# Turning the row maxima with one transpose and placing them by transfers, in an attention and expert-layer kernel

## The chip, the cores and the metric

The kernel runs on one core of a Trainium2 chip. A core has five engines with a queue of instructions each: TensorE (PE in the profile; PEld is its loading of weights), VectorE (DVE), ScalarE (ACT), GpSimd (POOL) and SyncE (SP), which here only issues transfers (DMAs). Each engine takes its own queue in order and waits at semaphores for the others. SBUF is the working memory with 128 partitions, PSUM holds the matmul results in banks. The metric is the time on the device in microseconds: 559.02 us, the median of three runs (559.01 to 559.05).

## What is computed

A layer of attention and then a mixture of experts, each followed by a residual sum and a layer norm, on x of 2 x 1024 x 256, all in float32. What matters here is the attention: 16 query heads of 16 elements share 4 key heads, a bias that grows linearly with the key's position is added, a causal mask, then softmax:

```python
q = (x @ Wq).reshape(B, T, N_HEAD, HEAD_DIM).transpose(0, 2, 1, 3)
k = (x @ Wk).reshape(B, T, N_HEAD_KV, HEAD_DIM).transpose(0, 2, 1, 3)
v = (x @ Wv).reshape(B, T, N_HEAD_KV, HEAD_DIM).transpose(0, 2, 1, 3)
...
att = jnp.einsum('bhqd,bhkd->bhqk', q, k) * scale
...
att = att + alibi[None]
...
att = att + causal[None, None]
att = jax.nn.softmax(att.astype(jnp.float32), axis=-1).astype(q.dtype)
y = jnp.einsum('bhqk,bhkd->bhqd', att, v)
y = y.transpose(0, 2, 1, 3).reshape(B, T, C)
return y @ Wo
```

The second half routes each token to one of 8 experts (top 1) and adds a shared expert; the change touches of it only the place where its first loads are issued.

## The kernel before

**Tiles.** There are 2 batches of 8 query tiles with 128 queries each, 16 in all, worked through as tiles 0 to 7 of batch 0 and then 7 to 0 of batch 1 (`order`). For query tile qt there are qt + 1 key tiles, so 72 steps (b, qt, kt). Each step is two slots, one for each half h of the four key heads.

**The operands.** `qT[b]` holds the queries turned, [128 partitions, 4 repeats r, 1024 tokens]: each key head g owns 32 partitions, of which row 16 and on hold the 16 elements of a head, row 0 (`ROW_POS`) serves the position bias, and row 1 (`ROW_MAX`) is for the maximum. `kT[b]` has the matching rows, with ones in `ROW_MAX`. So a matmul over the 32 partitions adds whatever stands in the query's row 1 to every score.

**Scores twice.** The scores are computed once with queries on partitions (`start_s`, line 427, tile `s_ps`), only to find each row's maximum: `end_s` reduces them on DVE (`past`, line 446), and takes the block on the diagonal to `diag` on DVE (line 459) or ACT (line 461), POOL masks it, and DVE reduces it later as a "chore" (line 478). Row 1 of `qT` is zero for this. Then they are computed again with keys on partitions (`start_t`, line 519, tile `t_ps`), now with the negated maximum in row 1; `end_t` takes exp of them on ACT (`pT`, line 538), or for the diagonal block copies them (`pD`, line 541), masks on POOL and takes exp (line 555). `product` (line 565) multiplies by v.

**Between the two.** `join_maxima` (line 492) joins the partial maxima of a tile into `mneg` on DVE; `spread_maxima` turns them on PE (line 503) and adds them to a copy of the queries, `qS`, on DVE (line 507), which `start_t` reads.

**The order.** It is written out by hand: all five engines run in program order (`manual_schedule`). The maxima run ahead of the exponentials by `LEAD` = 10 units, which run first, among the projections of the remaining tokens (`do_q` and others, from `fill`). Then each slot is a burst of t and s matmuls in turn, t0, s0, t1, s1, followed by `gap`, with one product, the joining or spreading of maxima (`maxima`), one piece of the work behind a finished tile (`posts`: yq, ytp, o_ps, x1tp, lg) and one chore. For tile k with its first step at slot 2*first, `join_maxima` runs in the gap of slot 2*first - 4, `spread_maxima` in that of 2*first - 3; the bursts of slots 2*first - 2 and 2*first - 1 lie between it and the first t matmuls of the tile. A slot whose spreading put it into `with_chore` runs no chore. When the maxima are all done (`s_queue` empty), `wide_gap` puts pieces of the shared expert (gu_sh, dp_sh) between bursts.

**Buffers.** s_ps, t_ps and most other matmul results share one pool of 6 PSUM banks; yT has one bank, and mT shares the last one with yq, ytp, o_ps and others (tag "m").

**Transfers.** `do_q` (line 358) issues 8 DMAs of 64 KB on SP for each 512 tokens, 32 in all, from SBUF to `qT` within SBUF. Behind the `LEAD` units, SP issues the loads of the shared expert's weights (lines 932 to 934) and fills the DRAM tables `slot_x` and `more_x` with one empty row repeated (line 941). Their next instructions on SP are the stores of `z_sh` (line 764), at the end of the attention. ACT issues the loads of Wq, Wk and Wv at the start, and nothing else before the expert stage. `slot` starts at -10, so that the spreading of tile 0 falls in slot -3 (behind the query transfers of batch 1's first half, before those of its second) and of tile 1 in slot -1, behind all of them.

Of the kernel before, what the change touches and what calls it, by code (L numbers as in the profile page):

```python
# [9 lines left out]
F32 = mybir.dt.float32  # L10
I32 = mybir.dt.int32
# [5 lines left out]
P = 128  # L17
N_HEAD = 16
N_KV = 4
REP = N_HEAD // N_KV  # L20
HD = 16
PAD = 32
ROW_POS = 0
ROW_MAX = 1
# [21 lines left out]
def attn_moe_postln_kernel(  # L46
# [15 lines left out]
    nc = tc.nc  # L62
    B, T, C = x.shape
    E, _, F2 = gate_up.shape
    FF = F2 // 2
# [3 lines left out]
    NTT = B * QT  # L69
# [9 lines left out]
    ROW = C + 4  # L79
    NUM, WT = C, C + 1  # L80
# [10 lines left out]
    acon = attn_scope.enter_context(tc.tile_pool(name="acon", bufs=1))  # L91
# [19 lines left out]
    sh_gu = const.tile([P, KC, F2], F32, tag="sh_gu", name="sh_gu")  # L111
    sh_d = const.tile([P, FC, C], F32, tag="sh_d", name="sh_d")

    mnegs = []
    for i in range(2):
        m = acon.tile([P, REP, N_KV, PAD], F32, tag=f"mneg{i}", name=f"mneg{i}")
        nc.gpsimd.memset(m, 0.0)
        mnegs.append(m)  # L120
    ident = const.tile([P, P], F32, tag="ident", name="ident")
    make_identity(nc, ident)
    neg_half = const.tile([P, 1], F32, tag="neg_half", name="neg_half")
# [25 lines left out]
    for g, slope in enumerate(alibi_slopes()):  # L149
# [14 lines left out]
        out=causal,  # L164
        in_=causal,
# [9 lines left out]
    for b in range(B):  # L175
# [15 lines left out]
        out=before,  # L191
        in_=ones,
# [75 lines left out]
    with (  # L268
# [12 lines left out]
        qT, kT, xT = {}, {}, {}  # L281
# [5 lines left out]
        def own_tiles(b, xTb):  # L287
            xT[b] = xTb
            kT[b] = qkp.tile([P, T], F32, tag="kT", name=f"kT_{b}")
            qT[b] = qkp.tile([P, REP, T], F32, tag="qT", name=f"qT_{b}")  # L290

        def other_rows(b, i, copy):

            copy(qT[b][:, :, i : i + 512], qbias.unsqueeze(2).broadcast_to([P, REP, 512]))
# [13 lines left out]
        def bank(name):  # L308
            return ps_st.tile([P, 512], F32, tag="st", name=name)


        def turn_x(b, i):
            if b not in xT:

                xTb = ptp.tile([P, KC, T], F32, tag="pT", name=f"xT_{b}")
                own_tiles(b, xTb)
                for j in range(0, T, 512):
                    other_rows(b, j, nc.gpsimd.tensor_copy)
            for c in range(KC):
                tp = bank("xtp")  # L320
                for j in range(4):
                    nc.tensor.transpose(tp[:, ts(j, P)], xs[:, b * QT + i + j, ts(c, P)], ident)
                nc.scalar.copy(xT[b][:, c, i * P : (i + 4) * P], tp)

        def do_kv(b, i):
            cols = slice(i * P, (i + 4) * P)
            pj = bank("kpj")
            project(pj, b, wk_of, cols)
            nc.vector.tensor_add(kT[b][:, cols], pj, kaug[:, cols])
            pv = bank("vpj")[:, : 4 * N_KV * HD].rearrange("p (j g d) -> p j g d", j=4, d=HD)  # L330
            for j in range(4):
                for c in range(KC):
                    nc.tensor.matmul(
                        pv[:, j].rearrange("p g d -> p (g d)"),
                        lhsT=xT[b][:, c, ts(i + j, P)],
                        rhs=wv_sb[:, c, :],
                        start=(c == 0),
                        stop=(c == KC - 1),
                    )
            nc.scalar.copy(vs[b][:, i : i + 4, :, 0:HD], pv)  # L340

        def do_q(b, i):


            cols = slice(i * P, (i + 4) * P)
            stage = ptp.tile([P, N_KV, 512], F32, tag="pT", name="q_all")[:, :2]
            for m in range(2):
                pj = bank("qpj")
                project(pj, b, wq_of(m), cols)
                if (b, i) == (0, 0) and m == 1:  # L350
                    nc.vector.tensor_copy(stage[:, m], pj)
                else:
                    nc.scalar.copy(stage[:, m], pj)
            to = qT[b].rearrange("p (m r) t -> p r m t", r=2)
            for r in range(2):
                for g in range(N_KV):
                    row = (r * N_KV + g) * HD
                    nc.sync.dma_start(
                        out=to[g * PAD + ROW_HEAD : g * PAD + ROW_HEAD + HD, r, :, cols],
                        in_=stage[row : row + HD],  # L360
                    )
# [15 lines left out]
        def first_projections():  # L377

            own_tiles(0, xTp.tile([P, KC, T], F32, tag="xT", name="xT_0"))
            cols = slice(0, 512)  # L380
            warm = bank("warm")
            zeros = mnegs[0].rearrange("p r g d -> p (r g d)")
            for i in range(2):
                nc.tensor.matmul(warm, lhsT=zeros[:, :P], rhs=zeros, start=True, stop=True)
            for c in range(KC):
                tp = bank("xtp0")
                for j in range(4):
                    nc.tensor.transpose(tp[:, ts(j, P)], xs[:, j, ts(c, P)], ident)
                nc.scalar.copy(xT[0][:, c, cols], tp)
            other_rows(0, 0, nc.scalar.copy)  # L390
            other_rows(0, 512, nc.gpsimd.tensor_copy)
            do_q(0, 0)
            do_kv(0, 0)
            turn_x(*halves[0])
            do_kv(*halves[0])
# [9 lines left out]
                done += n  # L405
            return [(b, qt, *u) for u in units]

        rowmax, parts = {}, {}

        def start_s(unit, h, j):  # L410
            b, qt, r0, nr, key, n = unit
# [69 lines left out]
                    )  # L481
                )

        qS = {}

        def join_maxima(b, qt):

            for c in [c for c in chores if c[1] == (b, qt)]:
                chores.remove(c)
                c[2]()  # L490
            past = rowmax.pop((b, qt))[1]
            nc.vector.tensor_reduce(
                mnegs[qt % 2][:, :, :, ROW_MAX].rearrange("p r g -> p g r"),
                past[:, :, :, : len(parts[b, qt])],
                AX.X,
                ALU.min,
            )

        def spread_maxima(b, qt):

            mT = ps_m.tile([P, REP, P], F32, tag="m", name="mT")
            for r in range(REP):
                nc.tensor.transpose(
                    mT[:, r, :], mnegs[qt % 2][:, r].rearrange("p g d -> p (g d)"), ident
                )
            q = mp.tile([P, REP, P], F32, tag="qS", name="qS")
            nc.vector.tensor_add(q, qT[b][:, :, ts(qt, P)], mT)
            qS[b, qt] = q
            with_chore.add(slot)


        probs, yTs = {}, {}
# [1 line left out]
        def start_t(b, qt, kt, h, j):  # L514
            g = h * HALF + j
            rows = slice(g * PAD, (g + 1) * PAD)
            tp = bank("t_ps")
            return tp, [
                lambda: nc.tensor.matmul(  # L519
                    tp,  # L520
                    lhsT=kT[b][rows, ts(kt, P)],
                    rhs=qS[b, qt][rows].rearrange("p r q -> p (r q)"),
                    start=True,
                    stop=True,
                )
            ]
# [252 lines left out]
        slot = 0  # L779
# [3 lines left out]
        chores, with_chore = [], set()  # L783
# [116 lines left out]
        def last_gap():  # L900
# [9 lines left out]
                tail.pop(0)()  # L910
            slot += 1

        first_projections()
        rps = ps_m.tile([P, KC, E], F32, tag="m", name="rps")
        for c in range(KC):
# [4 lines left out]
        slot = -LEAD  # L920
# [8 lines left out]
                fill.pop(0)[1]()  # L929
            gap(0)  # L930

        nc.sync.dma_start(out=sh_gu[:, :, :FF], in_=sh_gate.rearrange("(c p) f -> p c f", p=P))
        nc.sync.dma_start(out=sh_gu[:, :, FF:], in_=sh_up.rearrange("(c p) f -> p c f", p=P))
        nc.sync.dma_start(out=sh_d, in_=sh_down.rearrange("(c p) n -> p c n", p=P))

        empty = shp.tile([P, ROW], F32, tag="th", name="empty")
        nc.gpsimd.memset(empty, 0.0)
        nc.gpsimd.memset(empty[:, NUM : NUM + 1].bitcast(I32), NTT * P)
        for to in (slot_xt, more_xt):
            n = to.shape[1]  # L940
            nc.sync.dma_start(out=to, in_=empty.unsqueeze(1).broadcast_to([P, n, ROW]))

        for n, (b, qt, kt) in enumerate(steps):
            last = n + 1 == len(steps) or steps[n + 1][:2] != (b, qt)
# [6 lines left out]
            if s_queue:  # L951
                unit = s_queue.pop(0)
                for h in range(2):

                    t, s = [], []
# [9 lines left out]
            else:  # L965

                t = [[start_t(b, qt, kt, h, j) for j in range(HALF)] for h in range(2)]
# [19 lines left out]
    with (  # L987
# [310 lines left out]
        rows = {e: fetch(e, nc.sync) for e in range(2)}  # L1298
        ws[3] = load(3)
        shared_down(2, h)  # L1300
        for i in range(2):

            d = sh_gu[:, i].rearrange("p (f c) -> p f c", f=FC)
# [16 lines left out]
        for i, w in enumerate(works):  # L1320
# [30 lines left out]
        n = nc.values_load(  # L1351
            how_many[0:1, 0:1],
            min_val=0,
            max_val=NO * QU,
            skip_runtime_bounds_check_because="a sum of quarters, at most NO * QU by their definition",
        )
# [54 lines left out]
```

## Time and profile before

| | |
|---|---|
| median of 3 runs | 559.02 us |
| the profiled execution | 559.09 us, its span 557.4 us |
| PE busy | 535.5 us (96%), 3330 matmuls |
| DVE busy | 341.0 us (61%) |
| ACT busy | 262.5 us (47%) |
| POOL busy | 153.2 us (27%) |
| mean granted clock of PE | 0.992 |
| mT transposes, line 503 | 64, 273 ns each (median, overlapping) |
| qS additions, line 507 | 16, 678 ns each |
| t_ps matmuls, line 519 | 576 records, 167.6 us |
| s_ps matmuls, line 427 | 896 records, 186.2 us |

An f32 matmul shows as two records, and matmuls on different groups of 32 partitions run beside each other, so the durations of single ones overlap; how long a group of them holds PE is read from its start to the start of the next group. A row of the timeline gives the start in us from the span's beginning, the duration in us, the engine ("q" behind it means its sequencer, for instance a DMA's issue), the line, the operation, the tiles it writes and reads, and how many in sequence are merged; behind it, in brackets, the engine's idle time before it and what ended that. A row for one tile's instructions gives the shortest, median and longest duration in ns. A DMA's issue is not its landing: the end of a transfer is seen in the small completion writes among the DMA packets of the trace.

### The profile page before, as it was taken

Reading aid. Unit: us, or ns where it says so; the run is one execution under the profiler, and the core shown is the slowest. Engines: PE = TensorE matmul, PEld = TensorE weight load, DVE = VectorE, ACT = ScalarE, POOL = GpSimd, SP = SyncE. Lnnn points to the kernel's source line nnn. Section 1 sums busy time; section 2 is a strip of 40 time slices with the busy share of each in tenths; the row PEclk is TensorE's granted clock in tenths of the full one; section 3 lists DMA queues with packets and bytes.
Section 4 is the critical chain, followed back from the end, with each engine's and each line's share of the span. In section 5 each row is a group of like instructions: output and inputs, shape, how many; then the busy total and the mean of one; then the engine's idle time right before and its main releaser. Section 6 shows DMA issues by size and latency. Waiting matters only on the chain.

```text
span 557.4 us, 8797 instructions
## 1 busy us (share of the span) xinstructions
PE 535.5 (96%) x3330; PEld 292.3 (52%) x3330; DVE 341.0 (61%) x808; ACT 262.5 (47%) x500; POOL 153.2 (27%) x183
## 2 busy tenths in 40 slices
PE   8999999999999999999999999999999989999982
PEld 4664444543333344444335544544756578888761
DVE  2389987787687678677967873334354227444442
ACT  3432876666676766666576765555211111111110
POOL 5310412201020202010432030141102034768652
PEclk9999899999999999999999999999999999999997
DMA  6222770000000000000100000010109676795110
GB/s 207 40 35 34 201 237 2 1 1 1 2 1 0 2 1 1 1 1 2 49 30 1 1 0 2 20 57 1 38 9 340 224 259 217 214 376 174 63 52 19
DMA packets 27136, 40.63 MB, mean 73 GB/s; under 512 B 3614, under 2 KB 20932, under 8 KB 27088
## 3 DMA queue, kind: packets, MB, share of 16 engines
q1 hardware_dynamic: 21472, 31.67, 18.2%
q0 software_dynamic: 3168, 6.34, 3.3%
q10 hardware_dynamic: 2448, 1.99, 1.2%
q8 instruction: 28, 0.46, 0.4%
q14 instruction: 20, 0.16, 0.1%
HBM read 27.70 MB, written 12.58 MB: 72 GB/s over the span
## 4 chain that ended last, share of the span: by engine, by line
PE 78%; issue 8%; DMA 4%; POOL 3%; DVE 3%; ACT 2%; POOLq 0%; ACTq 0%; DVEq 0%
PE t_ps L519 21%; PE yT L565 11%; PE s_ps L427 10%; PE gp L1207 4%; PE up L1207 4%; PE dp L1225 4%; DMA out_dram<-zt,row 4%; PE gu_sh L733 3%; PE qpj L298 3%; PE o_ps L612 2%; PE dp_sh L753 2%; PE kpj L298 1%; PE yq L593 1%; PE gp L1113 1%; PE lg L641 1%
## 5 line engine op out<-in xcount | busy, mean ns | idle before, releaser
L427 PE MATMUL s_ps<-kT,qT 32*128 32x512 f32 (+2 forms) x896 | 186.2, 473 | 1.2 <-ACT diag L461 0.8
L446 DVE TENSOR_REDUCE past<-s_ps 128x1 f32<-128x512 f32 (+3 forms) x256 | 148.1, 619 | 52.2 <-PE s_ps L427 45.6
L519 PE MATMUL t_ps<-qS,kT 32*128 32x512 f32 x576 | 167.6, 643 | 0.3 <-DVE diag L459 0.3
L538 ACT ACTIVATE pT<-t_ps 128x512 f32<-128x512 f32 x224 | 121.5, 599 | 76.6 <-PE s_ps L427 52.7
L427 PEld LDWEIGHTS s_ps<-kT,qT 32*128 32x128 f32 x896 | 80.5, 185 | 14.7 <-ACT pT L538 3.3
L519 PEld LDWEIGHTS t_ps<-qS,kT 32*128 32x128 f32 x576 | 51.9, 184 | 56.2 <-issue 31.3
L543 POOL TENSOR_SCALAR_AFFINE_SELECT pD<-pD 128x1024 f32<-128x1024 f32 x32 | 34.9, 1096 | 93.3 <-ACT pD L541 93.2
L565 PE MATMUL yT<-pT,v 128*32 128x512 f32 (+1 forms) x472 | 60.3, 583 | 0.0
L235 POOL TENSOR_TENSOR rstd<-rstd,neg_half 128x1 f32<-128x1 f32 x33 | 18.9, 575 | 126.6 <-DVE rstd L234 92.8
L464 POOL TENSOR_SCALAR_AFFINE_SELECT diag<-diag 128x1024 f32<-128x1024 f32 x16 | 17.5, 1097 | 96.0 <-ACT diag L461 96.0
L733 PE MATMUL gu_sh<-x1T,sh_gu 128*128 128x512 f32 x96 | 43.6, 597 | 0.2 <-DVE h_sh L742 0.2
L541 ACT COPY pD<-t_ps 128x512 f32<-128x512 f32 x64 | 34.3, 597 | 20.0 <-PE s_ps L427 13.7
L478 DVE TENSOR_REDUCE past<-diag 128x4 f32<-128x512 f32 x64 | 42.5, 679 | 0.0
L1215 ACT ACTIVATE sg<-gp 128x512 f32<-128x512 f32 x16 | 9.6, 598 | 53.5 <-PE gp L1207 43.6
L555 ACT ACTIVATE pD<-pD 128x1024 f32<-128x1024 f32 x32 | 34.2, 1069 | 0.7 <-POOL pD L543 0.7
L461 ACT COPY diag<-s_ps 128x128 f32<-128x128 f32 (+2 forms) x64 | 24.0, 378 | 22.0 <-DVE past L446 19.1
L459 DVE TENSOR_TENSOR diag<-s_ps,causal 128x128 f32<-128x128 f32 (+2 forms) x64 | 26.6, 418 | 8.9 <-PE s_ps L427 8.6
L565 PEld LDWEIGHTS yT<-pT,v 128*32 128x32 f32 x472 | 9.3, 108 | 37.5 <-issue 35.5
L733 PEld LDWEIGHTS gu_sh<-x1T,sh_gu 128*128 128x128 f32 x96 | 17.5, 190 | 18.5 <-issue 17.2
L1152 POOL DMA_INDIRECT zt<-z_dram,row x17 | 17.5, 1029 | 26.7 <-DMA z_dram<-z 21.8
L241 POOL DMA_INDIRECT slot_x<-xs,slots x16 | 16.0, 1002 | 31.3 <-DVE slots L711 27.6
L1207 PE MATMUL gp<-slot_xT,wgu 128*128 128x256 f32 x96 | 23.0, 382 | 1.2 <-ACT slot_xT L1176 1.2
(178 smaller groups left out, 667.3 us busy)
## 6 DMA issues: line engine op xcount, KB each, us to landing
wgu<-_L_ffn_gate_up_proj_dram SPq DMA_DIRECT2D x10, 1024.0 KB
wd<-in_L_ffn_down_proj_dram SPq DMA_DIRECT2D x10, 512.0 KB
slot_x<-empty SPq DMA_DIRECT2D x1, 2080.0 KB
xs<-in_L_attn_x_dram SPq DMA_DIRECT2D x4, 512.0 KB
qT<-q_all SPq DMA_DIRECT2D x32, 64.0 KB
x1T<-_L_ffn_gate_up_proj_dram SPq DMA_DIRECT2D x2, 1024.0 KB
more_x<-empty SPq DMA_DIRECT2D x1, 1820.0 KB
row<-slot_x ACTq DMA_DIRECT2D x6, 260.0 KB
```

The source lines that it names most:

```text
L427: lambda r=r: nc.tensor.matmul(sp[:, r * n * P : (r + 1) * n * P], lhsT=qT[b][rows, r0 + r, ts(qt, P)], rhs=kT[b][rows, key * P : (key + n ...
L446: nc.vector.tensor_reduce(past[:, h * HALF + j, heads, parts[b, qt][key]], sp[j][:, :, : past_n * P], AX.X, ALU.max, negate=True,)
L459: nc.vector.tensor_tensor(to, block, bound, ALU.min)
L478: lambda g=g: nc.vector.tensor_reduce(past[:, g, :, 0], diag[:, g], AX.X, ALU.max, negate=True),
L519: lambda: nc.tensor.matmul(tp, lhsT=kT[b][rows, ts(kt, P)], rhs=qS[b, qt][rows].rearrange("p r q -> p (r q)"), start=True, stop=True,)
L538: nc.scalar.activation(p[:, j], tp[j], AF.Exp)
L541: nc.scalar.copy(p[:, j], tp[j])
L543: nc.gpsimd.affine_select(out=p, in_=p, pattern=[[0, HALF * REP], [1, P]], compare_op=ALU.is_ge, fill=MASKED, base=0, channel_multiplier=-1,)
L555: lambda: nc.scalar.activation(p, p, AF.Exp),
L565: nc.tensor.matmul(yTs[b, qt][g * PAD : (g + 1) * PAD, cols], lhsT=vs[b][:, kt, g, :], rhs=p[:, g, cols],  start=start and part != 1, stop ...
L733: nc.tensor.matmul(gu[k], lhsT=sh_gu[:, c, col : col + P], rhs=x1T[:, c, ts(tb, TB)], start=(c == 0), stop=(c == KC - 1),)
L1207: nc.tensor.matmul(dst[:, j], lhsT=ws[e][0][:, c, col : col + P], rhs=xT[:, c, :], start=(c == 0), stop=(c == KC - 1),)
```

## The change

The four transposes of a tile's maxima become one: `mneg` is now a small tile [128, 4 r, 4 g], made anew for each query tile, with all 16 heads beside each other, and one transpose turns it to 16 rows of 128 queries. DVE copies these rows from PSUM to `mrows` in SBUF. Four DMAs on SP, one for each r, bring 4 rows of 512 bytes each into `ROW_MAX` of the four heads in `qT`. `qS` and its addition are gone; the t matmuls read `qT` itself, in four pieces of 128 queries, 4 KB apart. The slot is no longer put into `with_chore`.

The loads of the shared expert's weights and the filling of the two tables move from SP's queue to ACT's, at the same place of the program. Making the empty row moves ahead, before the first projections, and the memsets of two padded `mneg` tiles become one of a tile `zeros` for the warming matmuls.

```diff
-    mnegs = []
-    for i in range(2):
-        m = acon.tile([P, REP, N_KV, PAD], F32, tag=f"mneg{i}", name=f"mneg{i}")
-        nc.gpsimd.memset(m, 0.0)
-        mnegs.append(m)
+    zeros = acon.tile([P, 512], F32, tag="zeros", name="zeros")
+    nc.gpsimd.memset(zeros, 0.0)
...
             past = rowmax.pop((b, qt))[1]
+            mneg = mp.tile([P, REP, N_KV], F32, tag="mneg", name="mneg")
+            mnegs[b, qt] = mneg
             nc.vector.tensor_reduce(
-                mnegs[qt % 2][:, :, :, ROW_MAX].rearrange("p r g -> p g r"),
+                mneg.rearrange("p r g -> p g r"),
...
         def spread_maxima(b, qt):
 
-            mT = ps_m.tile([P, REP, P], F32, tag="m", name="mT")
+            heads = N_KV * REP
+            mT = ps_m.tile([P, P], F32, tag="m", name="mT")
+            nc.tensor.transpose(
+                mT[:heads], mnegs.pop((b, qt)).rearrange("p r g -> p (r g)"), ident
+            )
+            rows = mp.tile([heads, P], F32, tag="mrows", name="mrows")
+            nc.vector.tensor_copy(rows, mT[:heads])
+            to = qT[b].rearrange("(g d) r t -> g d r t", d=PAD)
             for r in range(REP):
-                nc.tensor.transpose(
-                    mT[:, r, :], mnegs[qt % 2][:, r].rearrange("p g d -> p (g d)"), ident
-                )
-            q = mp.tile([P, REP, P], F32, tag="qS", name="qS")
-            nc.vector.tensor_add(q, qT[b][:, :, ts(qt, P)], mT)
-            qS[b, qt] = q
-            with_chore.add(slot)
+                nc.sync.dma_start(
+                    out=to[:, ROW_MAX, r, ts(qt, P)], in_=rows[r * N_KV : (r + 1) * N_KV]
+                )
...
-                    rhs=qS[b, qt][rows].rearrange("p r q -> p (r q)"),
+                    rhs=qT[b][rows, :, ts(qt, P)],
...
+        empty = shp.tile([P, ROW], F32, tag="th", name="empty")
+        nc.gpsimd.memset(empty, 0.0)
+        nc.gpsimd.memset(empty[:, NUM : NUM + 1].bitcast(I32), NTT * P)
         first_projections()
...
-        nc.sync.dma_start(out=sh_gu[:, :, :FF], in_=sh_gate.rearrange("(c p) f -> p c f", p=P))
-        nc.sync.dma_start(out=sh_gu[:, :, FF:], in_=sh_up.rearrange("(c p) f -> p c f", p=P))
-        nc.sync.dma_start(out=sh_d, in_=sh_down.rearrange("(c p) n -> p c n", p=P))
-
-        empty = shp.tile([P, ROW], F32, tag="th", name="empty")
-        nc.gpsimd.memset(empty, 0.0)
-        nc.gpsimd.memset(empty[:, NUM : NUM + 1].bitcast(I32), NTT * P)
+        nc.scalar.dma_start(out=sh_gu[:, :, :FF], in_=sh_gate.rearrange("(c p) f -> p c f", p=P))
+        nc.scalar.dma_start(out=sh_gu[:, :, FF:], in_=sh_up.rearrange("(c p) f -> p c f", p=P))
+        nc.scalar.dma_start(out=sh_d, in_=sh_down.rearrange("(c p) n -> p c n", p=P))
         for to in (slot_xt, more_xt):
             n = to.shape[1]
-            nc.sync.dma_start(out=to, in_=empty.unsqueeze(1).broadcast_to([P, n, ROW]))
+            nc.scalar.dma_start(out=to, in_=empty.unsqueeze(1).broadcast_to([P, n, ROW]))
```

More of the change, by code (lines that the diff above doesn't have):

```diff
@@ L381, in first_projections @@
             warm = bank("warm")
-            zeros = mnegs[0].rearrange("p r g d -> p (r g d)")
             for i in range(2):
@@ L406, in s_units @@
             return [(b, qt, *u) for u in units]
-        rowmax, parts = {}, {}
+        rowmax, parts, mnegs = {}, {}, {}
         def start_s(unit, h, j):
@@ L482, in end_s @@
                 )
-        qS = {}
         def join_maxima(b, qt):
```

## The prediction

> **What bounds the kernel now.** I read the table of engines first: TensorE (PE) is busy for 96% of the span, and the chain of waits gives PE 78%. That average hides which stage pays, so I went to the timeline around each of the 16 places where a query tile's maxima are turned (numbered 0 to 15 here in the order of the work). One of them, tile 5:
>
> ```profile
> 118.78 0.66 PE L503 MATMUL mT<-ident,mneg 128*128 128x128 f32 x4
> 119.37 0.69 PE L519 MATMUL t_ps<-qS,kT 32*128 32x512 f32 x1
> ...
> 119.01 1.29 DVE L446 TENSOR_REDUCE past<-s_ps 128x2 f32<-128x512 f32 x2 [0.43 <-PE s_ps L427]
> 120.22 0.68 DVE L507 TENSOR_TENSOR qS<-qT,mT 128x512 f32<-128x512 f32 x1
> ```
>
> The four transposes hold PE from 118.78 to 119.37, 0.59 us. The burst of score matmuls behind them then takes 1.69 us, to 121.05, where an unhindered burst takes 1.07. Its last score matmuls can't go before the two reductions from 119.01 give banks back: there are six banks and a burst takes four. So in this stage a shorter PE piece is followed by a longer wait. Elsewhere a two-transpose piece (0.37) is followed by a burst of 1.56, a four-transpose piece (0.59) by one of 1.34: 1.93 both times.
>
> Next I read SyncE's (SP's) queue, which is to carry the new transfers, and beside it ScalarE (ACT), which gets the loads:
>
> ```profile
> 11.32 49.39 SPq L358 DMA_DIRECT2D qT<-q_all  x32
> 60.76 0.59 SPq L932 DMA_DIRECT2D sh_gu<-L_ffn_shared_gate_w_dram  x1
> 61.39 0.48 SPq L933 DMA_DIRECT2D sh_gu<-n_L_ffn_shared_up_w_dram  x1
> 61.91 0.47 SPq L934 DMA_DIRECT2D sh_d<-L_ffn_shared_down_w_dram  x1
> 62.48 0.45 SPq L941 DMA_DIRECT2D slot_x<-empty  x1
> 62.98 5.81 SPq L941 DMA_DIRECT2D more_x<-empty  x1
> ...
> 56.87 0.27 ACT L461 COPY diag<-s_ps 128x128 f32<-128x128 f32 x1 [0.86 <-DVE past L446]
> 57.04 1.08 ACT L541 COPY pD<-t_ps 128x512 f32<-128x512 f32 x2
> ```
>
> SP is busy with the query transfers until 60.7. The fifth of the loads takes 5.81 us to issue. On SP nobody waits for that, since its next work comes at 357 us. On ACT the same place in program order lies between the two lines at 56.87 and 57.04.
>
> **What is removed.** Three of four transposes a tile: four hold PE 0.53 us in the last stage (343.24 to 343.77), two 0.31, so one about 0.19, and 0.34 is saved. Times 16 this is 5.4 us if all of it is on the path. It isn't where the next burst waits for banks. I count it in full for tiles 13 to 15, whose next burst is 1.07 (1.0 us), and half for tiles 2 and 4, with bursts of 1.10 and 1.07 (0.3): **gain 1.3 us**. VectorE (DVE) loses an addition of 0.68 and gets a copy of 16 x 128 from PSUM, priced by the 128-column operation of line 459 at 0.28: 0.40 x 16 = 6.4 us less DVE work. In the fence above the next reductions (120.81) would still wait for matmuls, so I count none of it. A maxima reduction of 0.68 may now stand in that slot, behind the copy: nothing, it only comes earlier.
>
> **What is added on every tile.** Copy, then four transfers of 2 KB on SP, then the first matmul of the tile, two bursts later. Issue: transfers of the queries follow each other by 0.635 us, the plain two-dimensional stores by 0.40:
>
> ```profile
> L764 SPq DMA_DIRECT2D z_dram<-z_sh x12: 319/345/618, 357.3 to 427.9; - x12
> L358 SPq DMA_DIRECT2D qT<-q_all x32: 585/592/1972, 11.3 to 58.7; - x32
> ```
>
> The new ones have two dimensions, so I take 0.40. Landing: by the trace's packet records the completion writes of a z_sh store end 1.36 us after its issue begins (357.27 to 358.63), of a query transfer 2.0 (25.25 to 27.2, and 29.70 to 31.78); I take 1.4. From copy's end: 0.05 to reach SP + 3 x 0.40 + 1.4 = 2.65 us. The copy ends 0.40 before the addition did, so the matmul is late if it follows the addition's end by less than 2.25. Before, that distance was, tiles 0 to 15: 4.8, 2.0, 3.1, 1.7, 2.8, 2.6, 3.5, 2.8, 3.3, 3.0, 2.4, 2.8, 3.6, 5.8, 5.6, 4.8. Tile 3 is late by 0.5; the rest are covered by the two bursts, tile 1 apart. At 0.635 and 1.75 (limit 3.3) nine tiles are late, 5 us in all. **Cost 0.8 us**, ends 0 and 5. Here the Trainium skill (DMA: Bandwidth & Descriptors, "Rules for kernel authors") speaks against the change: many small transfers should become one, since below 64 KB one pays mostly overhead. The rows agree that size hardly matters; one transfer would land 3 x 0.40 = 1.2 us sooner. But by the rows the four are hidden at most tiles, so obeying the rule would save tile 3's half microsecond, while reading it as a cost of 1.2 a tile would charge 19 us.
>
> Reads of qT in four pieces 4 KB apart: DVE's strided read of yq (line 597, 0.425) is 7 ns above the contiguous addition of line 615 (0.418): nothing. Other matmuls that read qT don't wait for the new writes: query transfers were issued into qT from 25.25 to 30.3 while score matmuls on it ran from 24.49, none waiting for a DMA. On POOL two memsets (0.42) come earlier and one of 0.53 goes; its next copy waits for DVE at 8.83: nothing.
>
> **What is moved, and the largest term.** Five issues go to ACT, ahead of the copies at 57.04. On SP they took 60.76 to 68.79, 8.0 us: four of about 0.5, then 5.81 in which the issuer is held while the first three loads are still landing (completion writes of sh_d end at 68.2). The queued bytes are the same on ACT, and it now begins while the last 8 query transfers still run, until 60.7: I add 1.1. ACT is then free at about 57.1 + 9.1 = 66.2. At the start of the kernel ACT's own loads show that its next instruction waits for the issue: the third ends at 2.44, the table load starts at 2.47. Queued behind are the copies that empty the banks of the first probabilities; PE stops at the next burst's second t_ps matmul, which needs such a bank, and DVE and POOL run dry behind it. ACT worked without a pause from 58.9 to 69.3, so it can't catch up there; I grant 1.0 afterwards. **Cost 8.1 us.**
>
> The skill (same page, "Issuing engines are not separate DMA queues") has another rule: issuing from several engines only saves the sequencer's time, usually small beside the DMA. Read as a price, that makes five issues of 0.5, 2.5 us of ACT; the row makes 8.0. I take the row, because it is the same five transfers.
>
> **Tile 1** has its own trouble: its four transfers stand on SP behind the last query transfers, so issue starts at 60.7, the last at 61.9, landing at 63.3 or later; before, its matmuls started at 59.67. That is 3.6 us, but inside ACT's 8 and not added. **Tile 2** sends while the loads still fill the DMA engines (share 1.09 at 69 to 73 us). ACT's row loads took 2.4 us to land on quiet engines and 6 to 8 beside weight loads on the other queue; with one packet an engine and transfer I take 1.9 us more against a cover of 0.9: **1.0 us**, ends 0 and 4. A pause of 9 us also brings back the granted clock of 0.50, seen before from 60.15 to 63.56; that stretch was already half speed and ACT-bound, so 0.
>
> **Sum.** 559.09 is the profiled execution (span 557.4 and 1.7 around it), 0.07 above the median shown. 559.1 + 8.1 + 0.8 + 1.0 - 1.3 = 567.7; less the 0.07, rounded: **567.5 us**.
>
> **Rivals.** *Issue is short on ACT* (0.22). ACT's queue starts empty, and SP's 5.81 may owe something to what lay in SP's. Then ACT loses 2.5 us and tile 1's wait of 3.6 decides, covering it: 559.0 + 3.6 + 0.8 + 0.2 - 1.3 = 562.3. Against it: the query transfers had landed, but for a few, by 62.2, when the held issue began.
>
> *Every tile's rows are late* (0.16): the main case with query-like pitch and landing, +4.2 more: about 572. For it: same kind of transfer, into the same tile. Against it: three dimensions there, 64 KB each.
>
> *Faster* (0.12): the place is the burst behind the transposes. If the DVE time removed lets the banks go earlier, PE's 5.4 us are kept, and what six of these places (tiles 5 to 9 and 11) take above the usual 1.93 goes too, 1.7; if ACT's issues cost only 2.5, with tile 1's rows landing within that pause: 559.0 - 7.1 + 2.5 + 0.8 = 555.2. It decides once ACT's pause is below about 6.3 us. Against it: the reductions at 119.01 precede the addition, so removing that frees no bank.
>
> **How the numbers follow.** Main case 0.50 (565 to 571). The range 560.8 to 574 takes nearly all of it, most of the short-issue case and most of the late-rows case, leaving out the faster one: 0.8. Faster by over 0.2% (about 1.1 us, the least a measurement of this kernel tells from no change): 0.11; within: 0.02, from the edges of the short cases; slower: 0.87.
>
> **What would show it.** Right: more_x's issue on ACT of 5 us or more, a PE pause of some 8 us from about 57, lower clock after it, and from 80 us on tiles at the old pace, with gaps only at tile 3's place. Wrong: ACT's five issues end by 60; bursts behind the single transpose shrink by a third of a microsecond; or first t_ps matmuls wait for the row transfers at most tiles.

## The result and the profile after

The changed kernel takes **572.69 us** (median of 4 runs, 572.22 to 573.09) against 559.03 (559.01 to 559.12) for the kernel before: 1.0232 times as long, 95% interval 1.0212 to 1.0253. The profiled execution took 572.22 us, with a span of 570.4, 13.0 more than before; its mean granted clock is 0.975, before 0.992.

The start of each query tile's transposes in the trace after, less that in the trace before, shows where time is lost or won:

| place | after minus before, us |
| --- | --- |
| transposes of tile 0, tile 1 | +0.25, +0.26 |
| first t_ps matmul of tile 1 | +12.61 (72.28 against 59.67) |
| transposes of tile 2, 3, 4 | +13.09, +14.21, +14.42 |
| tiles 5 to 13 | +14.35 to +14.31 |
| tile 14, tile 15, first t_ps matmul of tile 15 | +13.98, +13.65, +13.22 |
| end of the span | +13.0 |

So 12.4 us go at one place, 1.8 more up to tile 4, nothing over the long middle, and about 1.1 comes back in the last three tiles. The timeline of the changed kernel around that place (start and length in us, engine, line, what runs; in brackets the idle time just before and what ended it), for SP, then ACT, then PE:

```profile
54.54 7.30 SPq L354 DMA_DIRECT2D qT<-q_all  x8
61.94 0.57 SPq L505 DMA_DIRECT2D qT<-mrows  x1
63.92 0.55 SPq L505 DMA_DIRECT2D qT<-mrows  x1
64.57 0.50 SPq L505 DMA_DIRECT2D qT<-mrows  x1
66.89 0.50 SPq L505 DMA_DIRECT2D qT<-mrows  x1
...
57.13 0.37 ACTq L933 DMA_DIRECT2D sh_gu<-L_ffn_shared_gate_w_dram  x1
58.07 0.63 ACTq L935 DMA_DIRECT2D sh_d<-L_ffn_shared_down_w_dram  x1
58.74 0.61 ACTq L938 DMA_DIRECT2D slot_x<-empty  x1
64.23 2.52 ACTq L938 DMA_DIRECT2D more_x<-empty  x1
66.79 1.07 ACT L539 COPY pD<-t_ps 128x512 f32<-128x512 f32 x2 [9.39 <-DMA qT<-q_all]
...
67.42 2.07 PE L422 MATMUL s_ps<-kT,qT 32*128 32x128 f32 x14 [7.38 <-ACT pD L539]
72.28 1.19 PE L517 MATMUL t_ps<-qT,kT 32*128 32x512 f32 x1 [2.78 <-DMA qT<-mrows]
```

Two things hold PE here, and they overlap. ACT's copies, which stood at 57.04, resume at 66.79: PE waits 7.38 us for them. Four issues take 2.2 us; the fifth first waits until 64.21, when the sixth of the eight query transfers, a transfer of the other queue, lands, and then takes 2.52. But after PE has its banks back it stops again, 2.78 us, for the maxima of tile 1. The four issues of its rows are not 0.6 apart, as elsewhere, and they start late: SP waits between them, and ahead of the last query transfer. Its waits, in the view of waits (total, times, longest, in us), are for transfers whose data neither the rows nor the query transfer use:

```profile
SPq L354 <- DMA sh_gu<-L_ffn_shared_gate_w_dram: 2.2, 1, 2.2
SPq L505 <- DMA sh_d<-L_ffn_shared_down_w_dram: 1.8, 1, 1.8
SPq L505 <- DMA sh_gu<-n_L_ffn_shared_up_w_dram: 1.4, 1, 1.4
```

The semaphore events say why: the transfers of SP and of ACT take their completion semaphores from the same eight (numbers 100, 102 and 104 to 109), in turn. A transfer that comes to a semaphore waits until its previous user has landed, on whichever queue that was. The last query transfer waits for the gate half of the shared weights (landed 61.24), so that the rows begin at 61.94 and not at 60.83, as they do below without the loads. The second row waits for the up half (63.86), the fourth for sh_d (66.82). The fourth's packets then move only at 70.96 to 71.15, 4.1 us after its issue.

The windows of the changed kernel behind it (stretch, length, busy us and count of PE, PEld, DVE, ACT, POOL; granted clock, DMA share, GB/s):

```profile
61.00:65.00 4.00, 0.00 (x0) 0.00 (x0) 0.00 (x0) 0.00 (x0) 0.00 (x0) 0.50 1.05 283
69.00:73.00 4.00, 1.22 (x8) 0.75 (x9) 1.28 (x2) 1.87 (x3) 2.16 (x3) 0.50 1.10 336
73.00:77.00 4.00, 4.00 (x16) 1.37 (x8) 2.57 (x5) 2.50 (x4) 1.09 (x1) 0.50 1.02 314
77.00:81.00 4.00, 4.00 (x19) 0.81 (x17) 2.87 (x6) 2.98 (x5) 1.09 (x1) 0.50 0.04 10
```

From 61 to 65 no engine computes. From 73 to 81 PE is busy without a gap, at half the clock: it was granted 0.50 from 60.57 to 81.05, 20.5 us, where before it was 3.4 (60.15 to 63.56). At its end the changed kernel lags by 14.5 us (a burst starts at 81.22, at 66.73 before), so the 1.8 us between tile 1 and tile 4 lie here.

Far from this place, the changed kernel's timeline at tile 5 (its transpose stood at 118.78 before) and in the last stage:

```profile
133.13 0.28 PE L498 MATMUL mT<-ident,mneg 128*16 128x128 f32 x1
133.34 0.69 PE L517 MATMUL t_ps<-qT,kT 32*128 32x512 f32 x1
...
135.40 1.06 PE L563 MATMUL yT<-pT,v 128*32 128x512 f32 x8
...
133.36 1.29 DVE L441 TENSOR_REDUCE past<-s_ps 128x2 f32<-128x512 f32 x2 [0.43 <-PE mT L498]
134.56 0.27 DVE L502 COPY mrows<-mT 16x128 f32<-16x128 f32 x1
...
357.55 0.27 PE L498 MATMUL mT<-ident,mneg 128*16 128x128 f32 x1
357.75 1.14 PE L517 MATMUL t_ps<-qT,kT 32*128 32x512 f32 x8
```

At tile 5 the turning holds PE for 0.21 us (133.13 to 133.34) in place of 0.59, and the burst behind it, up to the product at 135.40, takes 2.06 in place of 1.69: 2.27 in all, both times. The two reductions that give banks back still end at 134.65. In the last stage the hold goes from 0.53 to 0.20 and the burst stays at 1.07, so there the third of a microsecond is kept. The rows of the new transfer and copy in the view of tiles (duration in ns min/median/max, first and last start in us):

```profile
L505 SPq DMA_DIRECT2D qT<-mrows x64: 497/497/613, 50.2 to 392.9; - x64
L502 DVE COPY mrows<-mT x16: 267/269/279, 50.0 to 390.9; 16x128 f32<-16x128 f32 x16
```

An issue takes 0.50, and in quiet stages the four follow each other by 0.59.

### The profile page after: what moved, and what is told of

Its sections match the earlier page's. It is cut to its first block, busy times and chain, and to the rows that moved or that the text cites. A ratio compares the mean times of both kernels' runs of the same rounds, so it can differ in the third digit from the quotient of the medians.

```text
span 570.4 us, 8864 instructions
## 1 busy us (share of the span) xinstructions
PE 535.8 (94%) x3282; PEld 287.8 (50%) x3282; DVE 335.0 (59%) x808; ACT 262.6 (46%) x500; POOL 152.5 (27%) x182
## 5 line engine op out<-in xcount | busy, mean ns | idle before, releaser
L422 PE MATMUL s_ps<-kT,qT 32*128 32x512 f32 (+2 forms) x896 | 189.8, 479 | 8.7 <-ACT pD L539 7.4
L517 PE MATMUL t_ps<-qT,kT 32*128 32x512 f32 x576 | 170.5, 648 | 6.3 <-DMA qT<-mrows 4.3
L517 PEld LDWEIGHTS t_ps<-qT,kT 32*128 32x128 f32 x576 | 52.4, 185 | 65.0 <-issue 34.8
L1213 DVE TENSOR_TENSOR slot_h<-sg,up 128x512 f32<-128x512 f32 x16 | 11.0, 687 | 24.0 <-PE up L1204 24.0
```

Of the source, the lines that this page charges most:

```text
L422: lambda r=r: nc.tensor.matmul(sp[:, r * n * P : (r + 1) * n * P], lhsT=qT[b][rows, r0 + r, ts(qt, P)], rhs=kT[b][rows, key * P : (key + n ...
L517: lambda: nc.tensor.matmul(tp, lhsT=kT[b][rows, ts(kt, P)], rhs=qT[b][rows, :, ts(qt, P)], start=True, stop=True,)
```

## The experiments

The question was what made the 12.4 us at tile 1. Theory one (H): ACT is held by the five issues, above all the fifth, and all behind it waits. Theory two (W): tile 1's rows come too late, behind the query transfers and the loads, and would have held PE whatever ACT did. Each ratio is against runs of the kernel before that were taken with it; their medians are 559.21 to 559.42, single ones 558.7 to 562.4.

**The loads alone on ACT.** The kernel before, with its five loads issued there and nothing else changed:

```diff
-        nc.sync.dma_start(out=sh_gu[:, :, :FF], ...)
+        nc.scalar.dma_start(out=sh_gu[:, :, :FF], ...)
...  (the other four alike; empty is filled earlier)
```

> The kernel before with nothing but the five loads moved to ACT (and the empty row made earlier); four transposes and the addition stay. Theory H (ACT is held while it issues the loads, and everything behind it stops): ACT resumes its copies at about 66 instead of 57 us, the time is 567 to 570 us. Rival R (the row transfers that SP issues late, and that wait for the loads to land, make the loss): without them ACT's own pause costs less than 3 us, the time is at most 562 us.

568.24 us, 1.0163 times before (1.0133 to 1.0193). The timeline of this kernel, ACT:

```profile
59.57 7.54 ACTq L940 DMA_DIRECT2D more_x<-empty  x1
67.15 1.07 ACT L541 COPY pD<-t_ps 128x512 f32<-128x512 f32 x2 [9.55 <-DMA qT<-q_all]
```

With no rows at all, the fifth issue itself takes 7.54 us and waits at no semaphore; PE waits 6.5 for the copies. The hold alone costs 9 us. On SP the same issue took 5.81, and nobody noticed.

**The rows alone.** The changed kernel, with the five loads back on SP and issued much later, ahead of tile 6's first step:

```diff
-        nc.scalar.dma_start(...)  # five loads
         for n, (b, qt, kt) in enumerate(steps):
+            if n == first[0, 6]:
+                nc.sync.dma_start(...)  # the same five
```

> The changed kernel, its five loads on SP again but issued behind the row transfers of tile 6 instead of at 57 us. H: ACT isn't held, what is left is tile 1's row transfers, which stand on SP behind the last query transfers (about +3.6 us), and the shorter transposes at the end (-1.0): about 561.5 us. R: the row transfers of tile 1 were the loss, and they still stand behind the query transfers: 566 us or more.

563.42, 1.0076 (1.0046 to 1.0105). Its timeline at tile 1:

```profile
64.36 1.19 PE L517 MATMUL t_ps<-qT,kT 32*128 32x512 f32 x1 [4.74 <-DMA qT<-mrows]
```

The time lies between the two expectations. The rows issue from 60.83, when the last query transfer is out, and PE waits 4.74 us. That is the place priced at 3.6 in the prediction. The clock is 0.50 until 67.71.

**Later loads as a control.** The kernel before with only the loads moved, in the program, to tile 6 on SP:

> The kernel before with its five loads issued on SP at tile 6 instead of 61 us, as a control for the kernels with late loads. If the loads' place by itself is worth nothing: 559.0 us, within 0.4. If their bytes slow the tiles at 61 to 80 us: 1 us or more below.

559.33, 1.0000 (0.9989 to 1.0011). It matches the expectation and yet controls nothing, for its timeline has the loads where they were:

```profile
60.49 0.59 SPq L938 DMA_DIRECT2D sh_gu<-L_ffn_shared_gate_w_dram  x1
...
62.72 5.51 SPq L943 DMA_DIRECT2D more_x<-empty  x1
```

SP has no other work there in this kernel, so it comes to the moved loads as early as before. In "the rows alone" they stand behind the rows of tile 6 and do go out late, from 153.53. How much of that kernel's 4.2 us is the rows' must be read from its own trace. Its lag behind the kernel before is 0.30 at the transposes of tile 1 and 4.45 at those of tile 2, and then stays between 4.4 and 4.7 up to tile 13, past the loads at tile 6. So the loss lies at tile 1, and the loads cost nothing at their new place; what their absence from 61 to 80 us gives was not measured by itself.

**The query transfers behind the rows.** As "the rows alone", with the last 8 query transfers held back until tile 1's rows have gone:

```diff
+                    if (b, i) == halves[-1]:
+                        held.append(send)
+                    else:
+                        send()
...
+        for send in held:
+            send()
```

> As the kernel with late loads on SP, and besides the eight query transfers of the last 512 tokens are issued on SP behind tile 1's row transfers instead of ahead of them. H: both covers are restored, only the saving in the last stage remains: 558.0 us, 1.0 below before. R: the rows arrive late at the other tiles too (gaps of 0.1 to 0.6 us in the trace of the changed kernel): no better than before, 559 to 561 us.

560.91 (558.24 to 561.9, 14 runs), 1.0011 (0.9994 to 1.0028): no difference from before that these runs can tell, and short of the 558.0 I expected. The timeline and one window of it:

```profile
60.81 1.19 PE L523 MATMUL t_ps<-qT,kT 32*128 32x512 f32 x1 [1.50 <-DMA qT<-mrows]
...
61.00:65.00 4.00, 4.00 (x16) 1.70 (x16) 2.07 (x5) 2.12 (x5) 1.76 (x2) 0.50 0.60 101
```

A gap of 1.5 us is left, because the copy of tile 1's maxima stands behind reductions on DVE and begins only at 56.94. From 60.17, within that gap, the clock is 0.50 for 10.2 us, though PE is busy behind the gap. The runs near 558.2 have a mean clock of 0.992 or more, those above 561 of 0.984; what decides between them I did not try.

**The copy on ACT.** The same kernel, to get rid of that gap:

```diff
-            nc.vector.tensor_copy(rows, mT[:heads])
+            nc.scalar.copy(rows, mT[:heads])
```

> As the kernel with late loads and query transfers behind tile 1's rows, and the rows are copied from PSUM by ACT instead of DVE. In that kernel tile 1 still waited 1.5 us for rows, because the copy stood on DVE behind two reductions, 2.1 us after the transpose had ended. H: ACT is free there, the copy starts 1.3 us earlier, the wait goes, and the granted clock falls for a shorter time: 558.0 us, below the kernel before by 1. Rival: ACT's copy delays its exponentials, or the clock is low whatever the wait, and the time stays at 560 to 561 us.

560.66 (22 runs), 1.0019 (1.0007 to 1.0031). It failed: on ACT the copy begins at 57.19, no earlier, and a gap of 1.26 stays.

**Is it the place or the engine?** The query-transfers-behind-rows kernel, with its late loads on ACT in place of SP:

> As the kernel with late loads and the query transfers behind tile 1's rows, but the five loads are issued on ACT, at tile 6, where no query transfer is under way. H: ACT is held there too, 2.2 us for four issues and up to 5.8 for the fifth, and PE stops with it: 564 to 566 us. R, or a hold that came only from the query transfers of the early place: ACT's issues cost 3 us or less there, 558 to 561 us.

570.03, 1.0189 (1.0159 to 1.0219), more than the 564 to 566 expected. ACT's timeline at tile 6:

```profile
155.99 6.32 ACTq L949 DMA_DIRECT2D more_x<-empty  x1
162.35 1.07 ACT L545 COPY pD<-t_ps 128x512 f32<-128x512 f32 x2 [8.25 <-DMA sh_d<-L_ffn_shared_down_w_dram]
```

With quiet queues, far from the query transfers, the fifth issue takes 6.32 us: it is held by the loads issued just before it, not by what else lies in a queue. It ends about when sh_d, the third load, lands: at 162.31, with sh_d at 162.31; at 67.11 with the loads alone on ACT (67.33), at 66.75 in the changed kernel (66.82) and at 68.79 on SP before (68.55). With the loads on SP at tile 6, in the rows alone, it ends 1.5 us after that landing. The same fill issued alone, at 162.92 on SP in the next kernel, takes 0.44. What it waits for inside the issue no trace shows. A pause of 8.5 us on ACT costs the kernel 9.1, as at tile 1.

**The changed kernel without the fifth issue.** Only more_x's fill goes to SP at tile 6; four loads stay on ACT:

> The changed kernel with only the fifth transfer (filling more_x) taken off ACT and issued on SP at tile 6; the other four loads stay on ACT at 57 us. H (the fifth issue is what holds ACT): ACT's pause shrinks to 2.2 us, and tile 1 waits for its rows only behind the query transfers, as with late loads: about 563.4 us. Rival W (besides, tile 1's row transfers wait on SP for the loads on ACT to land, as the trace of the changed kernel has it for two of them): tile 1 starts at 67 to 69 instead of 64 us, 566 to 568 us.

571.57, 1.0203 (1.0177 to 1.0229), above both expectations. Its timeline, ACT and PE:

```profile
59.81 1.07 ACT L539 COPY pD<-t_ps 128x512 f32<-128x512 f32 x2 [2.07 <-PE t_ps L517]
...
71.94 1.19 PE L517 MATMUL t_ps<-qT,kT 32*128 32x512 f32 x1 [9.42 <-DMA qT<-mrows]
```

ACT is free 7 us sooner, and the kernel gains about 1, with intervals that overlap. PE now waits 9.42 us for the rows, whose second and fourth issue again wait for the up half (64.15) and for sh_d (66.98). W holds: in the changed kernel, the rows end last.

**The changed kernel with early rows.** Now the other one is taken away: the 8 query transfers go behind tile 1's rows, the loads stay on ACT.

> The changed kernel with only the eight last query transfers moved on SP behind tile 1's rows; all five loads on ACT at 57 us. H (ACT's hold sets the time): tile 1's rows land by 61 us, but ACT is still held to 66 or 67 us: 568 to 570 us, and what this is below the changed kernel is the share of the late rows. Rival R (late rows set the time): 561 to 563 us.

567.37, 1.0136 (1.0113 to 1.0158), a little under the 568 to 570 expected. The trace is of an execution of 569.60; it is 2.0 us behind the kernel before already at tile 0. Rows issue from 59.28 to 61.05; ACT's timeline:

```profile
67.49 0.37 ACTq L946 DMA_DIRECT2D more_x<-empty  x1
67.90 1.07 ACT L545 COPY pD<-t_ps 128x512 f32<-128x512 f32 x2 [8.73 <-DMA qT<-q_all]
```

ACT is held as long as before, here by waiting at a semaphore until the issue, with nothing left in its way (sh_d landed at 67.28), takes 0.37. PE waits 6.3 for it. So the hold alone is worth 8 us, and the late rows another 5.3 (572.7 less 567.4).

**The loads back on SP, where they were,** with the rows of every tile on the same queue:

> The changed kernel with the five loads on SP at their old place, behind tile 1's rows: the one part of the change undone. ACT isn't held. Tile 1 waits as with late loads (about +4). H: then tile 2's rows stand on SP behind the issue of more_x, and their bytes behind the loads in the same queue, which landed at 79 us in the kernel before: tile 2 starts at about 80 instead of 69 us, in all 569 to 573 us, so that moving the loads off SP was needed and ACT was the wrong place. Rival: loads on SP in front of the rows cost nothing beyond tile 1's wait: 563 us.

575.47, 1.0281 (1.0258 to 1.0305), above the 569 to 573 expected and the slowest of all. The timeline of PE:

```profile
63.96 1.19 PE L517 MATMUL t_ps<-qT,kT 32*128 32x512 f32 x1 [4.41 <-DMA qT<-mrows]
...
82.66 1.19 PE L517 MATMUL t_ps<-qT,kT 32*128 32x512 f32 x1 [7.91 <-DMA qT<-mrows]
```

more_x's issue holds SP from 64.94 to 71.38, and the rows of tile 2 stand behind it. Their first issue then takes 4.15 us itself, and the fourth row, issued at 76.92, lands at 82.56, behind the loads in the same queue: a second gap of 7.9 us. With the rows on SP, the loads had to leave that place on SP.

**The loads on POOL,** the changed kernel otherwise:

> The changed kernel with the five loads issued on POOL at the same place, whose transfers count in semaphores of their own. So tile 1's rows can't wait for a load to land, but the loads' bytes still fill the DMA engines beside them. If the waiting at shared semaphores made the rows late (they stood on SP until 66.9 us for it): the fourth row is issued at about 64, it needs up to 4 us to land under the load, tile 1 starts at 67 to 68 instead of 72 us, in all 567 to 568 us. If the bytes alone make them late: tile 1 starts at 71 us or later, 571 us or more. POOL's issue holds the diagonal masks too, at 1 us each up to 2 us more.

570.54, 1.0204 (1.0189 to 1.022). The timeline, POOL and PE:

```profile
62.51 1.10 POOL L938 DMA_DIRECT2D more_x<-empty  x1
...
69.49 1.18 PE L517 MATMUL t_ps<-qT,kT 32*128 32x512 f32 x1 [8.68 <-DMA qT<-mrows]
```

Here neither the engine is held (the fifth issue takes 1.10) nor do the rows wait for a load between their issues (61.37 to 63.28). Yet the fourth row's packets move at 68.13 to 68.50, 4.9 us after its issue, where on quiet engines it takes 1.15. The time lies between both expectations: of what was named, only the bytes of the loads are left to delay the rows here.

The four kernels set out tile 1's start step by step: 59.67 before; 64.36 with the query transfers ahead (+4.7); 69.49 with the loads' bytes beside (+5.1); 72.28 with the shared semaphores and ACT's hold as well (+2.8). The last two steps are no clean split, since the loads on POOL also start later than on ACT, at 58.87 for 57.13.

**The part that gains, alone.** The kernel before, loads untouched, with the new way for tiles 13 to 15 only:

```diff
+        by_rows = {(1, qt): None for qt in range(3)}
...
+            if (b, qt) in by_rows:
+                ...  # one transpose, copy, four transfers on SP
+                return
```

> The kernel before, with the new way (one transpose, copy, four row transfers) only for the last three tiles, 13 to 15, where the bursts behind the transposes don't wait for banks and 4.8 us or more lie between the addition and the first matmul; the loads stay where they were. Saving of 0.33 us for each: 558.0 us, 1.0 below before. If the rows are late there as well, or the saving is taken back by a later wait: 559 us or more.

558.30 (557.8 to 560.0, 21 runs) against 559.25: 0.9982 (0.9973 to 0.9991), **shorter than both kernels**. Its timeline at tile 13, and the window that was half speed before:

```profile
343.78 0.27 PE L510 MATMUL mT<-ident,mneg 128*16 128x128 f32 x1
343.98 1.14 PE L539 MATMUL t_ps<-qS,kT 32*128 32x512 f32 x8
...
61.00:65.00 4.00, 3.69 (x22) 1.72 (x19) 4.00 (x8) 4.00 (x8) 3.23 (x3) 1.00 0.65 165
```

Hold 0.20, burst 1.07: 0.33 us at each of three tiles. The second line says that the profiled run also lacked the low clock there, so of the span's 0.7 us not all need be the tiles'; the interval is the surer evidence.

**The middle too.** The same with the new way from tile 4 on:

```diff
+        by_rows = {(b, qt): None for b, qt in [(0, t) for t in range(4, QT)] + [(1, t) for t in range(QT)]}
```

> As the kernel with the new way for the last three tiles, but for the nine tiles before them too (4 to 15); tiles 0 to 3 keep the old way and the loads their old place. If in the middle stage the shorter transposes are worth nothing, because the next burst waits for banks all the same, and the gaps at the first matmuls of a tile take the place of other waits: 558.3 us, as with three tiles. If the shorter transposes pay 0.34 us each: 555.2 us. If the gaps (1.6 us over tiles 4 to 12 in the trace of the changed kernel) are lost time: 559.9 us.

558.22 against 559.42, 0.9982 (0.9968 to 0.9996). Nine more tiles bring nothing and cost nothing.

## Why the prediction came out as it did

The direction, the place and the range were right. The 567.5 is 5.2 us below the measured 572.7, which lies outside the main case (565 to 571), and the step that failed is the one on tile 1.

- **Tile 1: "inside ACT's 8 and not added".** This is what the missing 5.2 us are. The rows were put at a landing of "63.3 or later" and as 3.6 us late; PE got them at 72.28, 12.6 late, so they outlast ACT's hold (67.4 for PE) rather than hide in it. The working priced them on quiet engines and by SP's own queue. It left out the loads that start beside them (loads on POOL: tile 1 starts 5.1 later than with the rows alone) and the shared semaphores. With only the rows taken out of the way (the changed kernel with early rows) 567.4 is left, which is the forecast. That it agrees to 0.1 is luck, since its small terms below did not come out as they stand.
- **The hold of ACT, 8.1.** Right in its size, its price and its cause, the loads still landing: ACT was free at 66.79 for the 66.2 predicted, about when sh_d landed, and the loads alone on ACT cost 9. Its make-up differs: the fifth issue waits 4.9 us at a semaphore first and then takes 2.52, not the 5 or more named as a sign of being right. The price of 2.5 for the whole, which the prediction made of the Trainium skill's rule (DMA: Bandwidth & Descriptors, "Issuing engines are not separate DMA queues"), is refuted by 7.54 and 6.32 us in the two kernels with nothing in that issue's way but the transfers before it. The rule itself calls the time to initiate a transfer usually small beside the transfer, and more_x, with the loads alone on ACT, lands 19.6 us after its issue begins.
- **The granted clock, "so 0".** Wrong as a fact, small as a term: 20.5 us at 0.50. All that was lost between tile 1's start and tile 4 is 1.8 us, against the 1.0 that was to be *won* there in catching up. The Trainium skill (TensorE: Matmul & The Clock Gate, "What's actually happening") has a window of 3.4 us, and the low stretch before, 3.41, agrees; here it lasted six such windows, with PE busy in the last 8.8 us (from 72.28). How much of the 1.8 is the clock's is not isolated.
- **Rows on every tile, 0.8.** The sizes were too low: the pitch is 0.59, not 0.40, and from the copy's end to the first matmul it is at least 3.46 us, not 2.65. By its own table that should have made tiles late, and it did: besides tile 1, seven gaps of 0.05 to 1.34 at first t_ps matmuls, each ending 0.1 to 0.2 us after the fourth row lands, 1.6 us of them in tiles 4 to 12. (The table's nine late tiles at the longer pitch are eight without tile 1.) But from tile 4 to 12 the two traces run 223.28 and 223.17 us. The likely reason is that the gaps fall into time that the shorter transposes leave over; the kernel from tile 4 on shows that in the middle gaps and savings together come to nothing. The working didn't have that. At tile 3 it is a gap of 1.34 in place of 0.5.
- **Tile 2, 1.0.** No gap of this kind is seen there; the 1.1 lost between tiles 2 and 3 goes with the low clock (the burst takes 2.02 against 1.10).
- **PE's gain, 1.3.** 1.1 in tiles 13 to 15, as worked out (1.0), and shown alone by the version that keeps only this. The 0.3 of tiles 2 and 4 isn't to be seen. No gain in the middle, also as worked out: the reductions, not the transposes, release the burst.

Of the rivals, *Issue is short on ACT* fell on ACT, but its other half, that tile 1's rows decide, is what the changed kernel does. *Every tile's rows are late* had the measured number, 572, from the wrong place: the middle tiles cost nothing in the trace and in the kernel from tile 4 on. *Faster* needed the burst to shrink, and it stretched.

## What to carry to other kernels

Before moving transfers to an engine that computes, read how long the *last* issue of the group takes where it is now: 5.81 us on an otherwise idle SP announced ACT's pause, whatever the four before it say. When two delays start at one place, price each to its end with the other's traffic running, for the later end decides, and removing only the one that ends first (about 1 of 13 us here) shows almost nothing. A control needs its own trace: an issue moved to a later line of an otherwise empty queue goes out as early as before. And a saving that is kept only in some stages can be applied there alone: three tiles of sixteen gave the whole gain.

## What the runs showed of the hardware that I had not expected

- Transfers of different queues wait for each other through completion semaphores: SP's last query transfer and two of its rows waited until 61.24, 63.86 and 66.82 for loads on ACT's queue, and ACT's fifth load until 64.21 for a query transfer on SP's.
- A transfer of 2 KB within SBUF moves 1.15 us after its issue on quiet engines and 3.8 to 4.9 us after it beside loads on another queue (tile 1's rows in the changed kernel and with the loads on POOL).
- Within a gap of only 1.5 us on PE (the query transfers behind the rows) the granted clock fell to 0.50, for 10.2 us, in a stage where PE was busy.
- The issue of the fifth load held its engine for 5.81 us on SP, 7.54 and 6.32 on ACT, to about the landing of the third load, but for 1.10 on POOL.
- Left open: what brings the low clock in some runs of one kernel and not in others, and what holds the fifth issue on SP and ACT.
